# A seventh of the aggregation by a second level of Strassen-Winograd: one of seven products split into seven of half size, in 13 of 16 units

## The chip, the cores and the metric

One core of a Trainium2 chip. The time is device microseconds of one execution, the median over several. The core's engines are named as the profile names them: PE is TensorE (matrix products into PSUM, the banks in which sums are held), DVE is VectorE, ACT is ScalarE, POOL is GpSimd and SP is SyncE. The last two only issue transfers in the stage that is looked at here. Every engine works through its own list of instructions in order; a list that waits holds everything behind it.

## What is computed

Two graph layers over 4096 nodes with 512 features. Everything is f32. The second layer is the larger part, and its last step, the aggregation, is what the change touches.

```python
def _L1_gnn_ref(x, adj, weight, bias, node_w, edge_w):
    ...
    node_att = jax.nn.softmax(x @ node_w, axis=0)
    h = x @ edge_w
    e = h @ h.T
    e = jnp.where(adj > 0, e, NEG_BIG)
    edge_att = jax.nn.softmax(e, axis=1)
    combined_att = node_att * edge_att
    support = x @ weight
    output = adj * combined_att @ support
    return output + bias
...
x = _layernorm(x + _L0_gnn_ref(x, adj, L0_gnn_weight), axis=-1)
x = _layernorm(x + _L1_gnn_ref(x, adj, L1_gnn_weight, ...), axis=-1)
```

## The kernel before

The kernel first does layer 0, then the scores e (4096 x 4096) block by block, which it stores in memory (`s_d`) with running row maxima and sums. The left-hand sides of the aggregation, the columns of the layer's input, are stored in memory too (`lop_d`), already combined for the scheme below. Then comes the stage of the change: it fills the profile from about 1078 us to the end.

The aggregation is cut into 16 units, `Aggregate(g, r)`, with g the outer and r the inner of two indices from 0 to 3. In the code units count n = 0 to 15. Unit (g, r) takes a square of 2 x 2 blocks of attention, each 512 x 512: the block rows r and r + 4, the block columns g and g + 4. A block lies in a buffer of 128 partitions x 4 x 512 (1 MB). There are 13 such buffers, `slot` and `lent`, handed out by `take()` in the order in which they were given back to `free`.

A unit multiplies the 2 x 2 square by a 2 x 2 left-hand side with seven products in place of eight (Strassen's scheme in Winograd's form). The right operands are the blocks r11, r21, r22 and four combinations t1 to t4 of them; the left operands are seven 512 KB slices of `lop_d[r]`, loaded on SP's queue into four buffers `lop` (L883). Each product m has two halves h, and each half is four matmuls of 128x512 into one PSUM bank `ps` (L887) out of a pool of six. After it, VectorE adds the bank to a running sum `total[m, h]` in `over` (L891); where r = 0 there is nothing to add to, and ScalarE copies (L889). Over the four r of one g these seven sums grow; then they are joined (L913), multiplied by the layer's weight (`Finish`, L969, matmuls of 128x256 into `po`), added to the input rows (L980), normalised and stored. That work for group g is queued in `todo` and handed out piece by piece among the products of the next group.

While unit n runs on TensorE, unit n + 1 is prepared, in steps (`steps`) that are handed out one or so after each half product by `between()`: loads of four score blocks on POOL's queue (`load`, L790), loads of four adjacency blocks (`mask`, L797), for each block a shift by the row maximum on VectorE (L803) and its exponential on ScalarE (L804), a weighing by the adjacency in four pieces on VectorE (`weigh`, L810), and last the four combinations (`combine`, L819 to L827). An adjacency buffer is given back after its weighing, and the next adjacency block is loaded then. At the end of a group `panel` makes the row maxima and factors for the next one; it turns them with four transposes on TensorE (L769), through one of two banks of another pool.

A scheduler sets the final order on each engine, from the order in which the code issues the work. So the lists of the built programs are read here, and not the code alone.

Of the kernel before, what the change touches and what calls it, by code (L numbers as in the profile page):

```python
# [11 lines left out]
F32 = mybir.dt.float32  # L12
# [6 lines left out]
P = 128  # L19
# [9 lines left out]
def kernel(  # L29
# [13 lines left out]
    nc = tc.nc  # L43
# [3 lines left out]
    W = 512  # L47
    NG = N // W
    BG = W // P
    HB = NB // 2  # L50
    HG = NG // 2
    HD = D // 2
# [6 lines left out]
    dram = ctx.enter_context(tc.tile_pool(name="dram", bufs=1, space=bass.MemoryType.DRAM))  # L59
# [16 lines left out]


    lop_d = [dram.tile([P, 7, BG, HD], F32, name=f"lop_d{g}") for g in range(HG)]

# [74 lines left out]
    with (  # L156
# [184 lines left out]
        with tc.manual_schedule(engines={mybir.EngineType.DVE, mybir.EngineType.Activation}):  # L341
            for n in range(NB):
                b = n // 2 + n % 2 * HB
# [58 lines left out]
        count = [0]  # L402
# [248 lines left out]
    class Couple:  # L651
# [38 lines left out]
        def quad(self, q, between):  # L690
# [56 lines left out]
            between()  # L747
            yield

    panels = {}  # L750

    def panel(A):

        cols = slice(A * BG, (A + 1) * BG)
        nm = small.tile([P, BG], F32, name="nm")
        nc.vector.tensor_reduce(nm, nmax_c[:, cols, :], AX.X, ALU.min)
        d = small.tile([P, BG, NG], F32, name="d")
        nc.vector.tensor_tensor(d, nm.unsqueeze(2).to_broadcast([P, BG, NG]), nmax_c[:, cols, :], ALU.subtract)
        nc.scalar.activation(d, d, AF.Exp)
        nc.vector.tensor_mul(d, d, sum_c[:, cols, :])  # L760
        f = pan.tile([P, BG], F32, name="f")
        nc.vector.tensor_reduce(f, d, AX.X, ALU.add)
        nc.vector.reciprocal(f, f)
        nc.vector.tensor_mul(f, f, node_att[:, cols])
        spread = rows.tile([P, BG, P], F32, name="spread", tag="rows")
        nc.vector.tensor_copy(spread, nm.unsqueeze(2).to_broadcast([P, BG, P]))
        pt = ps_tr.tile([P, BG, P], F32, name="ptm", tag="tr")
        for i in range(BG):
            nc.tensor.transpose(pt[:, i, :], spread[:, i, :], ident)  # L769
        if A % HG:  # L770
            free_e.append(panels[A - 1][1])
        mrow = take(free_e)
        nc.scalar.copy(mrow.rearrange("p (b w) -> p b w", w=P), pt)
        panels[A] = f, mrow
# [4 lines left out]
    class Aggregate:  # L779
# [46 lines left out]
                self.t4 = take()  # L826
                pinned[0](nc.vector.tensor_sub(self.t4, self.t2, r21))  # L827

        def steps(self):

            self.q, self.a, self.since = [None] * 4, [None] * 4, [None] * 8

            def begin():
                for n in range(2):
                    self.load(n)
                    self.mask(n)
                for n in range(2, 4):
                    self.load(n)

            yield begin  # L840
            yield lambda: self.shift(0)
            yield lambda: self.shift(1)
            for n in range(2):
                yield lambda n=n: self.weigh(n, n + 2)
                yield lambda n=n: self.shift(n + 2)
            yield lambda: self.weigh(2, None)
            yield lambda: self.weigh(3, None)
            for n in range(4):
                yield lambda n=n: self.combine(n)
# [23 lines left out]
                yield landed(n), lambda n=n: self.shift(n)  # L873
                yield landed(4 + n), lambda k=k, n=n: self.weigh(n, order[k + 2] if k < 2 else None)

        def main(self, between):
            r11, t1, r21, r22 = self.q
            total = sums[:, self.g % 2]
            last = self.g == HG - 1 and self.r == HG - 1
            for m in (0, 1, 5, 6, 4, 2, 3) if last else (0, 1, 2, 4, 6, 5, 3):  # L880
                rop = (lambda: r11, lambda: r21, lambda: r22, lambda: self.t4, lambda: t1, lambda: self.t2, lambda: self.t3)[m]()
                lop = lopp.tile([P, BG, HD], F32, name="lop")
                nc.sync.dma_start(lop, lop_d[self.r][:, m])  # L883
                for h in range(2):
                    ps = ps_mm.tile([P, W], F32, name="ps", tag="mm")
                    for c in range(BG):
                        nc.tensor.matmul(ps, lop[:, c, ts(h, P)], rop[:, c, :], start=(c == 0), stop=(c == BG - 1))  # L887
                    if self.r == 0:
                        nc.scalar.copy(total[:, m, h, :], ps)  # L889
                    else:  # L890
                        nc.vector.tensor_add(total[:, m, h, :], total[:, m, h, :], ps)  # L891
                    between()
                free.append(rop)
                if last:
                    for done in self.joins.get(m, ()):
                        join(self.g, done, nc.vector)
# [20 lines left out]
    class Finish:  # L917
# [26 lines left out]
        def pair(self, q, pool):  # L944
            sums_g = sums[:, self.g % 2]
            upper, lower = (sums_g[:, 2], sums_g[:, 4]) if self.half else (sums_g[:, 1], sums_g[:, 3])
            a, b = q, q + 2
            l11, l12, l21, l22 = (x[:, :, ts(i, P)] for i in (a, b) for x in (upper, lower))
            tag = "tr" if pool is ps_tr else "mm"
            bank, s = {}, []  # L950

            def combine():
                s.append(lopp.tile([P, 4, KD // 2, P], F32, name="left1", tag="lop"))
                s1, s2, s3, s4 = (s[0][:, n] for n in range(4))
                nc.vector.tensor_add(s1, l21, l22)
                nc.vector.tensor_sub(s2, s1, l11)
                nc.vector.tensor_sub(s3, l11, l21)
                nc.vector.tensor_sub(s4, l12, s2)

            def multiply(name, lop, rop, *to):  # L960

                first = name not in bank
                if first:
                    x = name == "x"
                    bank[name] = (ps_mm if x else pool).tile([P, HD], F32, name="po", tag="mm" if x else tag)
                po = bank[name]
                lop = lop if not isinstance(lop, int) else s[0][:, lop]
                for k in range(KD // 2):
                    nc.tensor.matmul(  # L969
                        po,  # L970
                        lop[:, k, :],
                        w1_r[rop][:, k, :],
                        start=(first and k == 0),
                        stop=(k == KD // 2 - 1),
                        skip_group_check=not first,
                    )
                f, _ = panels[self.A]
                for i, h in to:
                    xb = self.xbs[i][:, ts(h, HD)]
                    nc.vector.scalar_tensor_tensor(xb, po, f[:, i : i + 1], xb, ALU.mult, ALU.add)  # L980

            def half_stats(i, h):
                if self.last:
                    if i not in self.stats:
                        if not spare:
                            spare.append(take(free_e))
                        at = 64 * (self.half * BG + i)
                        self.stats[i] = spare[0][:, at : at + 12].rearrange("p (h s) -> p h s", h=2)
                    nc.vector.bn_stats(self.stats[i][:, h, :], self.xbs[i][:, ts(h, HD)])
                    if h == (0 if i == b else 1):  # L990
                        self.norm([i])

            yield combine
            yield lambda: multiply("y", l11, 0, (a, 0))
            yield lambda: (multiply("x", l12, 1, (a, 0)), half_stats(a, 0))
            yield lambda: multiply("y", 1, 5, (a, 1))
            yield lambda: multiply("z", 0, 4, (b, 1))
            yield lambda: (multiply("y", 2, 6, (b, 1)), half_stats(b, 1))
            yield lambda: (multiply("z", 3, 2, (a, 1)), half_stats(a, 1))
            yield lambda: (multiply("y", l22, 3, (b, 0)), half_stats(b, 0))  # L1000
# [92 lines left out]
        early_.popleft()[1]()  # L1093
    reclaim()
    todo = deque()


    over = big.tile([P, KD * N], F32, name="over", tag="large")
# [8 lines left out]

    for n, u in enumerate(blocks):
        nxt = blocks[n + 1] if n + 1 < len(blocks) else None
        first = deque()  # L1110
        pinned[0] = tc.keep_in_program_order if n == 0 else lambda ins: ins
        if n == 0:
            first.extend(f for _, f in early_)
            first.extend(lambda n=n: u.combine(n) for n in range(4))
        if nxt:
            first.extend(nxt.steps())
            if n:
                first.popleft()()
            if u.r == HG - 1:
                first.extendleft([lambda: panel(nxt.g + HG), lambda: panel(nxt.g)])  # L1120
# [6 lines left out]

        def between():
            count[0] += 1
            for queue, share in ((first, -(-len(first) // (15 - count[0]))), (todo, 1)):  # L1130
                for _ in range(min(share, len(queue))):
                    queue.popleft()()

        u.main(between)
        assert not first
        if u.r == HG - 1 and nxt:
            todo.extend(lambda g=u.g, n=n: join(g, n, nc.vector) for n in range(7))
# [4 lines left out]
    assert not todo  # L1142

    for e in ends_:
        for steps in zip(e.pair(0, ps_tr), e.pair(1, ps_mm)):
            for step in steps:
                step()

# [36 lines left out]
```

## Time and profile before

| what | us |
|---|---|
| median of 6 runs | 1957.35 |
| lowest and highest of them | 1954.27, 1960.07 |
| the profiled execution | 1954.27 |
| its span | 1952.5 |
| VectorE busy in it | 1386.9 |
| ScalarE busy in it | 694.2 |

The profiled execution is the lowest of the six, and its span is what the instructions cover; the rest of its time lies around them. A busy TensorE is not a TensorE at its peak, since matmuls are pipelined and the ends of their records are modelled: a row's mean (592 ns for 128x512) is longer than the step from one matmul to the next. An f32 matmul leaves two records. The costliest groups of the stage, with line, engine, operation, output and input, count, then busy time in us, mean ns, idle time before them and what ended it:

```profile
L887 PE MATMUL ps<-lent,lop 128*128 128x512 f32 x960 | 423.4, 592 | 0.0
L887 PE MATMUL ps<-slot,lop 128*128 128x512 f32 x832 | 365.7, 592 | 0.0
L891 DVE TENSOR_TENSOR over<-over,ps 128x512 f32<-128x512 f32 x168 | 114.1, 682 | 101.9 <-PE ps L887 101.9
L803 DVE CUSTOM_DVE_ANT_1 lent<-lent,line 128x2048 f32<-128x2048 f32 x32 | 73.1, 2287 | 26.2 <-DMA lent<-s_d 26.2
L803 DVE CUSTOM_DVE_ANT_1 slot<-slot,line 128x2048 f32<-128x2048 f32 x32 | 73.0, 2287 | 20.0 <-DMA slot<-s_d 18.7
```

The stage's transfers (queue, operation, count, size of one, median us from issue to landing):

```profile
lop<-lop_d SPq DMA_DIRECT2D x112, 512.0 KB, 3.9
slot<-s_d POOLq DMA_DIRECT2D x32, 1024.0 KB, 6.7
lent<-s_d POOLq DMA_DIRECT2D x32, 1024.0 KB, 7.4
```

### The profile page before, as it was taken

The page shows a single profiled execution, that of the slowest core. Times are in us where ns is not written, and L with a number is a line of the kernel's source. Part 1 is how long each engine was busy: PE and PEld are TensorE (multiplying, and loading weights), DVE is VectorE, ACT ScalarE, POOL GpSimd, SP SyncE. Part 2 cuts the span into 40 slices and gives each one's busy share as a digit, 9 for nine tenths or more (in the row PEclk, how much of TensorE's full clock was granted, in tenths as well). Part 3 has the DMA queues.
Part 4 walks back from the last instruction along what each step waited for, and adds up shares of the span by engine and source line. Part 5 has one row for each costly group of instructions (what it writes and reads, how often), then busy time and mean ns, then how long its engine had stood idle before and what let it go on. Part 6 is the DMA issues. An engine that isn't in the chain of part 4 may idle for free.

```text
span 1952.5 us, 18709 instructions
## 1 busy us (share of the span) xinstructions
PE 1939.3 (99%) x6314; PEld 1124.9 (58%) x6314; DVE 1386.9 (71%) x2154; ACT 694.2 (36%) x1134; POOL 326.1 (17%) x472
## 2 busy tenths in 40 slices
PE   9999999999999999999999999999999999999998
PEld 6888888888544445455555444445544555445545
DVE  7767666676774576567565896987769766988637
ACT  5433333333203576677677420221222220331100
POOL 0122222122441111011122211111111110211100
PEclk9999999999999999999999999999999999999999
DMA  9898888888385577578679977775777765776631
GB/s 312 296 326 311 294 324 312 303 318 309 122 298 191 183 263 296 197 272 284 240 297 326 336 279 267 257 251 192 249 247 262 246 244 192 282 248 215 215 97 43
DMA packets 134064, 497.75 MB, mean 255 GB/s; under 512 B 13904, under 2 KB 13904, under 8 KB 126288
## 3 DMA queue, kind: packets, MB, share of 16 engines
q0 software_dynamic: 70752, 260.08, 35.4%
q1 hardware_dynamic: 54864, 207.12, 31.8%
q10 hardware_dynamic: 8352, 29.36, 4.2%
q8 instruction: 50, 0.82, 0.2%
q14 instruction: 46, 0.38, 0.1%
HBM read 376.96 MB, written 119.54 MB: 254 GB/s over the span
## 4 chain that ended last, share of the span: by engine, by line
PE 93%; DMA 2%; issue 2%; DVE 1%; ACT 1%; POOL 0%; POOLq 0%; DVEq 0%; ACTq 0%
PE ps L887 39%; PE seven L699 12%; PE acc L371 11%; PE acc L370 11%; PE seven L98 5%; PE po L969 5%; PE pe L630 4%; PE pt L600 2%; DMA s_d<-slot 2%; PE acc L243 1%; PE pw L211 1%; PE pt L330 1%; ACT line L571 1%; PE acc L244 1%; PE idle L197 0%
## 5 line engine op out<-in xcount | busy, mean ns | idle before, releaser
L887 PE MATMUL ps<-lent,lop 128*128 128x512 f32 x960 | 423.4, 592 | 0.0
L370 PE MATMUL acc<-xw,hi 128*128 128x512 f32 x960 | 376.4, 392 | 0.0
L371 PE MATMUL acc<-xw,lo 128*128 128x512 f32 x960 | 374.2, 390 | 0.0
L887 PE MATMUL ps<-slot,lop 128*128 128x512 f32 x832 | 365.7, 592 | 0.0
L887 PEld LDWEIGHTS ps<-lent,lop 128*128 128x128 f32 x960 | 182.0, 190 | 205.4 <-issue 200.9
L887 PEld LDWEIGHTS ps<-slot,lop 128*128 128x128 f32 x832 | 157.8, 190 | 183.8 <-issue 179.4
L362 DVE TENSOR_TENSOR lo<-at,hi 128x1024 fp32r<-128x1024 f32 x120 | 146.9, 1224 | 85.2 <-ACT hi L360 85.2
L371 PEld LDWEIGHTS acc<-xw,lo 128*128 128x128 f32 x960 | 180.3, 188 | 37.1 <-DVE lo L362 0.3
L370 PEld LDWEIGHTS acc<-xw,hi 128*128 128x128 f32 x960 | 180.3, 188 | 36.8
L360 ACT CAST hi<-at 128x1024 fp32r<-128x1024 f32 x120 | 126.4, 1054 | 203.4 <-PE acc L370 151.0
L891 DVE TENSOR_TENSOR over<-over,ps 128x512 f32<-128x512 f32 x168 | 114.1, 682 | 101.9 <-PE ps L887 101.9
L804 ACT ACTIVATE lent<-lent 128x2048 f32<-128x2048 f32 x32 | 61.2, 1912 | 212.7 <-DVE lent L803 212.7
L630 PE MATMUL pe<-hT 128*128 128x512 f32 (+3 forms) x384 | 132.1, 486 | 0.0
L562 DVE CUSTOM_DVE_ANT_0 line<-lent,slot 128x512 f32<-128x512 bf16 x144 | 93.0, 687 | 45.9 <-ACT slot L640 23.0
L571 ACT ACTIVATE line<-line,nmax_c 128x512 f32<-128x512 f32 x160 | 114.8, 724 | 22.2 <-DVE nmax_c L562 22.1
L803 DVE CUSTOM_DVE_ANT_1 lent<-lent,line 128x2048 f32<-128x2048 f32 x32 | 73.1, 2287 | 26.2 <-DMA lent<-s_d 26.2
L699 PE MATMUL seven<-hT 128*128 128x512 f32 x192 | 89.8, 593 | 0.0
L804 ACT ACTIVATE slot<-slot 128x2048 f32<-128x2048 f32 x32 | 61.2, 1911 | 77.7 <-DVE slot L803 72.8
L630 PEld LDWEIGHTS pe<-hT 128*128 128x128 f32 x384 | 64.6, 191 | 41.4 <-issue 33.8
L803 DVE CUSTOM_DVE_ANT_1 slot<-slot,line 128x2048 f32<-128x2048 f32 x32 | 73.0, 2287 | 20.0 <-DMA slot<-s_d 18.7
L600 PEld LDWEIGHTS pt<-ident,lent 128*128 128x128 f32 x412 | 51.2, 141 | 52.9 <-issue 38.9
L601 ACT COPY slot<-pt 128x512 f32<-128x512 f32 (+3 forms) x126 | 69.5, 554 | 27.0 <-PE pt L600 23.2
(228 smaller groups left out, 2565.8 us busy)
## 6 DMA issues: line engine op xcount, KB each, us to landing
at<-in_adj_t_dram SPq DMA_DIRECT2D x60, 1024.0 KB, 7.0
lop<-lop_d SPq DMA_DIRECT2D x112, 512.0 KB, 3.9
lent<-in_adj_t_dram POOLq DMA_DIRECT2D x34, 1024.0 KB, 6.6
s_d<-slot POOLq DMA_DIRECT2D x33, 1024.0 KB, 7.0
slot<-s_d POOLq DMA_DIRECT2D x32, 1024.0 KB, 6.7
lent<-s_d POOLq DMA_DIRECT2D x32, 1024.0 KB, 7.4
slot<-in_adj_t_dram POOLq DMA_DIRECT2D x30, 1024.0 KB, 6.8
lent<-in_adj_dram SPq DMA_DIRECT2D x48, 512.0 KB, 5.1
```

The source lines that it names most:

```text
L98: nc.tensor.matmul(banks[bank][q], lop(m, q)[k], rop(m)[k], start=(first and k == 0), stop=(k == K - 1), skip_group_check=not first,)
L360: nc.scalar.copy(hi, aq)
L362: nc.vector.tensor_sub(lo, aq, hi.bitcast(F32))
L370: nc.tensor.matmul(acc, hi[:, c, :], xw[:, kb, :], start=(kb == 0), stop=False)
L371: nc.tensor.matmul(acc, lo[:, c, :], xw[:, kb, :], start=False, stop=(kb == NB - 1))
L571: nc.scalar.activation(line, line, AF.Exp, bias=nmax_c[:, b, c : c + 1], scale=-1.0, accum_out=sum_c[:, b, c : c + 1])
L630: nc.tensor.matmul(pe[:, lo * P :], hT[:, k, ts(A * BG + i, P)], hT[:, k, (B * BG + lo) * P : (B + 1) * W], start=(k == 0), stop=(k == KD ...
L699: nc.tensor.matmul(ps, left[m][:, k, q, :], right[m][:, k, :], start=(first and k == 0), stop=(k == KD // 2 - 1), skip_group_check=not first,)
L803: pinned[0](nc.vector._custom_dve(TENSOR_ADD_SAT, out=q, in0=q, in1=m, s0=0.0, s1=-HUGE))
L804: nc.scalar.activation(q, q, AF.Exp)
L887: nc.tensor.matmul(ps, lop[:, c, ts(h, P)], rop[:, c, :], start=(c == 0), stop=(c == BG - 1))
L891: nc.vector.tensor_add(total[:, m, h, :], total[:, m, h, :], ps)
```

## The change

In units 2 to 14 (`two`), product 0 of the seven, r11 by its left-hand side, is no longer done as two halves of four matmuls. It is cut once more into a 2 x 2 square and done by the same scheme with seven products of half size, each two matmuls of 128x256: 14 matmuls of 128x256 in place of eight of 128x512. The other six products stay and count 12 turns; after each turn one piece of the seventh is issued (`beside`).

- The right side: four differences of 128x2x256 on VectorE in turns 1 to 4, one of them in place (r12), three into a buffer `right` taken at the unit's start.
- The left side: the raw slice of `lop_d` is loaded on SP's queue into a buffer taken in turn 2, and its four combinations with it. The first time that an r comes up (units 2 to 5) the combinations are made on VectorE and stored to the new `lop2_d[r]`; the other nine times they are loaded from there.
- The seven half-size products come in turns 5 to 11. They run through two banks: y takes four of them on top of each other, and x and z, the two halves of the other bank, take the rest. After each one VectorE adds the running bank into a quarter of the sum of product 0; where r = 0, the first write of each quarter is a copy on ScalarE.
- To make room, the load of the next unit's fourth score block moves from the unit's start to turn 4.
- The six banks are made once and handed out by hand in turn (`next_bank`); while a half-size chain runs it holds two of them, and the other products turn through four. The panels' transposes and part of the last `Finish` go through the same ring. The steps of the next unit are spread over 12 turns, where it was 14.

```diff
+    def next_bank():
+        banks.rotate(-1)
+        return banks[-1]
...
+        def second(self, nxt):
...
+            r = self.q[0]
+            (r11, r12), (r21, r22) = [[r[:, k : k + h, c : c + w] for c in (0, w)] for k in (0, h)]
+            total = sums[:, self.g % 2, 0]
+            c = {f"{k + 1}{n + 1}": total[:, k, n * w : n * w + w] for k in range(2) for n in range(2)}
+            new = set(c) if self.r == 0 else set()
+            right = take()
...
+            def load():
+                left = l["buf"] = take()
...
+                nc.sync.dma_start(raw, lop_d[self.r][:, 0])
+                if not fresh:
+                    nc.sync.dma_start(left[:, h:, :], lop2_d[self.r])
...
+            def multiply(name, lop, rop, *to):
+                first = name not in bank
+                if first:
+                    if name == "z":
+                        bank["z"] = bank["x"][:, w:]
+                    else:
+                        bank[name] = banks.popleft()
+                ps = bank[name][:, :w]
...
+                for k in range(h):
+                    nc.tensor.matmul(ps, lop[:, k, :], rop[:, k, :], start=(first and k == 0), ...)
+                for n in to:
+                    if n in new:
+                        new.remove(n)
+                        nc.scalar.copy(c[n], ps)
+                    else:
+                        nc.vector.tensor_add(c[n], c[n], ps)
...
+            return {
+                1: [lambda: nc.vector.tensor_sub(t3, r22, r12)],
+                2: [load, lambda: nc.vector.tensor_sub(r12, r12, r11)],
+                3: [lambda: nc.vector.tensor_sub(t2, r22, r12)],
+                4: [(lambda: nxt.load(3)) if nxt else (lambda: None), lambda: nc.vector.tensor_sub(t4, r21, t2), combine],
+                5: [lambda: multiply("y", "11", r11, "11")],
+                6: [lambda: multiply("x", "12", r21, "11")],
+                7: [lambda: multiply("y", 2, t2, "12")],
+                8: [lambda: multiply("z", 1, r12, "22")],
+                9: [lambda: multiply("y", 3, t3, "22")],
+                10: [lambda: multiply("z", 4, r22, "12")],
+                11: [end],
+            }
...
-            for m in (0, 1, 5, 6, 4, 2, 3) if last else (0, 1, 2, 4, 6, 5, 3):
+            beside = self.second(nxt) if two else {}
+            turn = 0
+            for m in (0, 1, 5, 6, 4, 2, 3) if last else (1, 2, 4, 6, 5, 3) if two else (0, 1, 2, 4, 6, 5, 3):
...
-                    ps = ps_mm.tile([P, W], F32, name="ps", tag="mm")
+                    ps = next_bank()
...
+                    turn += 1
+                    if h:
+                        free.append(rop)
+                    for act in beside.get(turn, ()):
+                        act()
...
+        two = 2 <= n < len(blocks) - 1
```

## The prediction, made before the changed kernel ran

> **What bounds the kernel now.** I read the page's first part and its chain first, then windows of one unit and a bit (54.3 us) over the aggregation stage (1078 us to the end), then the chain in order of time, and last the rows that price what the change adds.
>
> ```profile
> span 1952.5 us, 18709 instructions
> PE 1939.3 (99%) x6314; PEld 1124.9 (58%) x6314; DVE 1386.9 (71%) x2154; ACT 694.2 (36%) x1134; POOL 326.1 (17%) x472
> PE 93%; DMA 2%; issue 2%; DVE 1%; ACT 1%; POOL 0%; POOLq 0%; DVEq 0%; ACTq 0%
> ```
>
> Three windows (columns: PE, PEld, DVE, ACT and POOL busy with counts, granted clock, DMA share, GB/s):
>
> ```profile
> 1349.90:1404.20 54.30, 54.30 (x147) 27.66 (x146) 38.92 (x64) 14.72 (x12) 10.34 (x16) 1.00 0.64 227
> 1458.50:1512.80 54.30, 54.30 (x128) 24.02 (x127) 53.80 (x60) 15.21 (x13) 7.49 (x10) 1.00 0.72 249
> 1512.80:1567.10 54.30, 54.30 (x148) 27.82 (x147) 42.33 (x50) 11.51 (x12) 5.99 (x8) 1.00 0.69 238
> ```
>
> TensorE has no idle time in the stage, at a granted clock of 1.00. VectorE is the runner-up: 38.9 us of 54.3 in an ordinary stretch, 53.8 where a group ends (there it also joins the seven sums and makes the panels), 42.3 after it. So work taken off TensorE shortens the kernel, as long as VectorE, which gets more, doesn't fall behind. The price of TensorE's work, from the chain in order of time (start, length, what):
>
> ```profile
> 1873.86 48.07 PE ps L887 x112
> 1921.92 19.87 PE po L969 x92
> L969 PEld LDWEIGHTS po<-over x128: 190/190/190, 1304.5 to 1936.9; 128*128 128x128 f32 x128
> L969 PE MATMUL po<-over x128: 379/379/379, 1304.9 to 1937.1; 128*128 128x256 f32 x128
> ```
>
> The first line is one whole unit: 7 products, 112 records (an f32 product of 128x512 leaves two), 0.429 us a record. The second is the same for 128x256: 0.216 us. The rows' 592 and 379 ns contain pipelining and are not the step.
>
> **TensorE's share of the change.** Removed in each of 13 units: one product of 16 records, 16 x 0.429 = 6.87 us. Added: seven half-size products, each of two products of 128x256, so four records: 28 x 0.216 = 6.05 us. Gain 0.82 us a unit, 10.65 us in 13. That the loads stay hidden is read from the row: a load takes 0.190 us and the step was 0.216. Break-even is 6.87 / 28 = 0.245 us a record.
>
> The Trainium skill, "TensorE: Matmul & The Clock Gate", Part 3 on packing small matmuls, states that a weight load overlaps matmuls in flight "only when row_grp differs"; all loads here are of the full 128x128. By that rule a unit would lose 28 x 0.406 - 16 x 0.619 = 1.46 us, the kernel 19 us. The trace says otherwise: 92 steps with their loads took 19.87 us, and 112 took 48.07.
>
> **VectorE's share.** The rows, with what stands in the order around them:
>
> ```profile
> 1477.01 2.28 DVE L824 TENSOR_TENSOR slot<-slot,slot 128x2048 f32<-128x2048 f32 x1
> 1479.22 0.68 DVE L891 TENSOR_TENSOR over<-over,ps 128x512 f32<-128x512 f32 x1
> 1479.81 2.28 DVE L827 TENSOR_TENSOR lent<-slot,slot 128x2048 f32<-128x2048 f32 x1
> 1482.02 0.68 DVE L891 TENSOR_TENSOR over<-over,ps 128x512 f32<-128x512 f32 x1
> 1482.61 2.28 DVE L803 CUSTOM_DVE_ANT_1 lent<-lent,line 128x2048 f32<-128x2048 f32 x1
> 1458.85 2.49 DVE L810 SCALAR_TENSOR_TENSOR slot<-lent,slot 128x512 f32<-128x512 f32 x4
> L955 DVE TENSOR_TENSOR left<-over 128x256 f32<-128x256 f32 x16 | 6.7, 417 | 0.0
> L1122 DVE TENSOR_TENSOR line<-over 128x512 f32<-128x512 f32 x1 | 0.7, 693 | 4.4 <-DMA over<-in_w_dram 4.4
> ```
>
> A unit with r > 0 holds 4 shifts (9.1), 16 weighs in fours (10.0), 4 combines (9.1) and 14 adds (9.5): 37.7 us of 48.07. Added: four differences of 2x256 columns, which is the shape of L1122, 4 x 0.69 = 2.8; eight adds of 128x256 out of PSUM, which no row has. Bounds: 0.42 (L955, same shape, from SBUF) and 0.48 (L980, 128x256 from PSUM with a scalar). I take 0.42, since L891 from PSUM (0.68) costs what L1122 costs from SBUF (0.69): 3.3 us. Removed: two adds of 0.68. Net 4.8 us (5.3 at the upper bound). With r = 0 four half sums are ScalarE copies, and two full ones left ScalarE before: net 2.8 + 1.7 = 4.5. The first use of each r (units 2 to 5) makes four left-hand sums, 1.7 us more. Over 13 units: 10 x 4.8 + 3 x 4.5 + 4 x 1.7 = 68 us. The twelve windows from 1187.0 to 1838.6 hold 505.6 us of VectorE in 651.6; so 574 in 641 remains, 90%. VectorE has room for it as a whole, not everywhere.
>
> **What waits.** Of six banks two go to the half products, so a bank is wanted again after three products, not five: 3 x 3.43 us and about two half products, 12 us, where it was 17. The reading of the group's end above shows adds of 0.68 every 2.8 us behind one combine or shift each; against 12 us that is cover. The two running half sums (y, and x whose other half is z) are tighter: each half product waits for the add of the one before it in its bank, two turns earlier, 2 x 3.43 + 0.86 = 7.7 us; between stand at most a shift, four weighs and an add (2.29 + 2.49 + 0.68 = 5.5). No wait, where the halves really come one a turn. In the built order of the changed kernel exactly one full product stands between any two halves in units 2 to 6, 9, 10, 13 and 14, and nearly so in 8 and 12 (one pair adjoins). In units 7 and 11, where groups 1 and 2 end, the panels crowd VectorE, and the last four halves come with half a product between them or less than one (0 to 0.75). From the four weighs that free the buffer of the adjacency until z's first half is added, the order has: reload of that buffer, four weighs, half add: 6.8 (page, slot<-in_adj_t, 1024 KB) + 2.49 + 0.42 = 9.7 us. On TensorE, in the same stretch, stand six matmuls of 128x512 (0.859 each, two records) and three half products (0.864), 7.75 us, before z's second half, which needs that add. Wait: 2.0 us each, 4.0 for both. Bounds: 0, if VectorE is ahead; with single reloads of this kind at 5.6 to 10.4 us in the trace, up to 5.6 each, 11 for both, all of the gain. I take the median.
>
> **What moves at no cost I can see.** The load of the fourth score block goes from the start of a unit to turn 4 on POOL's queue, into the buffer that the second product gives back: 4 x 3.43 = 13.7 us into the unit, landing 6.7 to 7.4 us later (page), 21 us. Its shift stands on VectorE at turn 6, 6 x 3.43 + two halves = 22.3 us. It is 1.3 us early; a slow landing (10.4) holds VectorE 2 us, with the adds behind it, and the ring of 12 us covers TensorE. On SP the half product's left side (512 KB) goes into the buffer that the first product frees, so SP waits up to 6.9 us, then a second load of 512 KB; the page's 3.9 us each makes 14.7 us, and the first half is wanted after turn 5, 17.2 us. Behind the wait stand the loads of later products; four buffers keep them three products ahead, 10 us or more. Nine extra loads and four stores of 512 KB are 6.8 MB of 497.75, DMA share 0.64 to 0.72. The panels' transposes move into the ring; the unit count and the last unit stay.
>
> **Sum.** 10.65 - 4.0 = 6.65 us. The profiled execution took 1954.27 us, 1.8 over its span, and is the lowest of six; it would become 1947.6. The median stands 3.1 us higher, 1957.35, so 1950.7 us is the forecast, 0.34%; 1946.7 if nothing waits. A measurement of this kernel can tell 0.2%, 3.9 us, from no change.
>
> **Rivals.** *The waits eat it.* The half sums' chain waits wherever a reload lands late, not in two units alone: 0.3 us to 1.1 us in each of 13 units (4 to 14 us), so 1951 to 1961, about 1957. For it: VectorE already waits for score blocks (L803 for s_d: 26.2 and 18.7 us in 64), and now half adds stand behind such waits. Against: the 7.7 us above.
> *VectorE becomes the bound.* Place: units 7/8 and 11/12, and 3/4. VectorE has 0.5 us left in 54.3 there, and gets 4.8 + 4.5 in about two units, some 9 us it must be late by; the halved ring holds 12, and the lateness also takes the next unit's operands. It decides from where the lateness passes 12 us, so if the added operations cost a third more than I take, or the backlog isn't gone (12 us idle in the next window, 7 after the change) by the next end. Then about 9 us show at each of three ends: 28 - 10.65, 17 us slower, 1975; with half of it 1961.
> *It doesn't do what it says:* the half products' step is above 0.245 us, because their operands come from strided quarters of buffers. Against: L969 reads quarters as well. 0.26 us would give 1957.35 + 13 x 0.4 = 1963.
>
> **How the numbers follow.** Forecast 0.66 (1946 to 1953.4), the waits eat it 0.18 (taken as within 3.9 us), VectorE 0.13, step 0.03. So faster 0.66, same 0.18, slower 0.16. The range runs from the gain without waits (10.65, and 0.7 for the median's own scatter) to the end of "same": 1946 to 1961; the forecast's own is 1946 to 1953.4.
>
> **What would show it.** Records of the halves 0.216 us apart; the stage's windows still at full PE; VectorE about 48 us of 54 in ordinary windows; PE's waits for VectorE a few us in all, at the ends of groups 1 and 2. Wrong if TensorE waits for a half add in most units, or if VectorE's full windows spread to two in a row with gaps in PE.

## The result, and the profile after

The changed kernel is a little slower: 1961.5 us median of 23 runs (1956.31 to 1973.74), beside 1957.22 us for the kernel before (48 runs). The ratio is 1.0024, 95% interval 1.0016 to 1.0032. The forecast was 1950.7. The profiled execution took 1957.13 us, 1.8 over its span, and is one of the shortest of the 23.

The page of the changed kernel, in the places shown of before: the engines, the shares of the chain that ended last, the costliest groups, the transfers.

```profile
span 1955.3 us, 19195 instructions
PE 1930.8 (99%) x6470; PEld 1153.5 (59%) x6470; DVE 1436.2 (73%) x2281; ACT 694.5 (36%) x1140; POOL 326.0 (17%) x472
PE 81%; DMA 7%; issue 6%; DVE 3%; POOL 1%; ACT 1%; POOLq 0%; DVEq 0%; SPq 0%; ACTq 0%
L981 PE MATMUL bank<-slot,lop 128*128 128x512 f32 x800 | 356.2, 592 | 0.0
L985 DVE TENSOR_TENSOR over<-over,bank 128x512 f32<-128x512 f32 x148 | 100.6, 681 | 67.7 <-PE bank L981 67.7
lop<-lop_d SPq DMA_DIRECT2D x99, 512.0 KB, 5.3
slot<-s_d POOLq DMA_DIRECT2D x37, 1024.0 KB, 7.4
lent<-s_d POOLq DMA_DIRECT2D x27, 1024.0 KB, 8.9
```

TensorE has less work, and the chain has left it: 81% of the span where it was 93%, and transfers have come in with 7%. VectorE's adds wait 67.7 us for banks where they waited 101.9, and the stage's transfers land 0.7 to 1.5 us later. The stage is as long as before: 868.8 us from the first record of its products (1079.9 us) to TensorE's last (1948.7), and the same in the kernel before (1077.3 to 1946.1). Counted from the starts of TensorE's records in the stage, against steps of 0.429 us for 128x512 and 0.215 for 128x256, it runs 10.7 us late in all in the changed kernel and 0.1 in the kernel before. So the 10.65 us that it has less to do came back as waits inside the stage. The windows of 54.3 us show where (the columns are those of before):

```profile
1404.20:1458.50 54.30, 51.69 (x155) 29.14 (x154) 35.55 (x56) 3.19 (x2) 4.49 (x6) 1.00 0.63 221
1458.50:1512.80 54.30, 53.10 (x146) 26.50 (x145) 49.38 (x64) 21.06 (x23) 11.10 (x17) 1.00 0.74 263
1512.80:1567.10 54.30, 54.30 (x158) 29.70 (x157) 51.98 (x65) 14.03 (x15) 6.74 (x9) 1.00 0.78 273
```

TensorE is full in most. It is short above all in the window with the second half of unit 6 and the first of unit 7, where VectorE is at 35.55 of 54.3 and so far from full, and a little in the next, with the rest of unit 7. The waits of TensorE in the stage, by what was waited for (us in total, times, longest), are one line; before, this view was empty:

```profile
PE bank L932 <- DVE over L945: 8.7, 5, 2.6
```

A half product (L932) waits five times for VectorE's add of a half product (L945): 2.61 us in unit 6, 1.95 in unit 10, 2.55 in unit 14, and 1.16 and 0.43 in units 7 and 11. The four records behind each wait take 1.13 us in the chain below, where they take 0.86 elsewhere, so the loss is some 10 us rather than 8.7. The chain of waits, in order of time, says what came ahead of the adds, in units 6 and 7:

```profile
1391.60 6.31 DMA out_dram<-xb
...
1398.19 0.53 POOL xb L1039
1398.72 8.68 DMA slot<-s_d
...
1407.42 2.29 DVE slot L815
1409.71 0.34 DVE over L945
...
1410.10 1.13 PE bank L932 x4
...
1415.53 0.86 PE bank L932 x4
...
1479.53 5.79 DMA slot<-in_adj_t_dram
...
1485.41 2.50 DVE slot L822 x4
1487.91 0.34 DVE over L945
...
1488.30 1.13 PE bank L932 x4
```

In unit 6 the last group's finished rows are stored (out_dram), the next input rows (xb) want the stored rows' buffers, and POOL's queue stands for the stores. Behind the rows stands the fourth score block, issued at 1398.72, 20.6 us into the unit (its first product starts at 1378.1). It lands 8.68 us later, VectorE shifts it, and only then does it reach the half add that TensorE wants. In unit 7 it is the chain that the prediction had named: reload of an adjacency block, four weighs, half add. The same view prices the halves: four records of 128x256 in 0.86 us.

### The profile page after: what moved, and what is told of

The parts are those of the page before. It is cut to its first block, busy times and chain, and to the rows that moved or that the text cites. A ratio compares the mean times of both kernels' runs of the same rounds, so it can differ in the third digit from the quotient of the medians.

```text
span 1955.3 us, 19195 instructions
## 1 busy us (share of the span) xinstructions
PE 1930.8 (99%) x6470; PEld 1153.5 (59%) x6470; DVE 1436.2 (73%) x2281; ACT 694.5 (36%) x1140; POOL 326.0 (17%) x472
## 4 chain that ended last, share of the span: by engine, by line
PE 81%; DMA 7%; issue 6%; DVE 3%; POOL 1%; ACT 1%; POOLq 0%; DVEq 0%; SPq 0%; ACTq 0%
PE bank L981 27%; PE seven L701 12%; PE acc L373 11%; PE acc L372 11%; PE pe L632 4%; PE seven L100 4%; PE bank L932 3%; PE po L1066 3%; PE pt L602 2%; DMA s_d<-slot 2%; DMA out_dram<-xb 1%; DMA slot<-s_d 1%; PE bank L1066 1%; PE acc L245 1%; PE pw L213 1%
## 5 line engine op out<-in xcount | busy, mean ns | idle before, releaser
L981 PE MATMUL bank<-slot,lop 128*128 128x512 f32 x800 | 356.2, 592 | 0.0
L981 PE MATMUL bank<-lent,lop 128*128 128x512 f32 x784 | 348.7, 592 | 0.0
L981 PEld LDWEIGHTS bank<-slot,lop 128*128 128x128 f32 x800 | 151.6, 190 | 162.8 <-issue 157.8
L981 PEld LDWEIGHTS bank<-lent,lop 128*128 128x128 f32 x784 | 148.8, 190 | 160.1 <-issue 154.7
L816 ACT ACTIVATE slot<-slot 128x2048 f32<-128x2048 f32 x37 | 70.6, 1910 | 260.2 <-DVE slot L815 249.7
L985 DVE TENSOR_TENSOR over<-over,bank 128x512 f32<-128x512 f32 x148 | 100.6, 681 | 67.7 <-PE bank L981 67.7
L815 DVE CUSTOM_DVE_ANT_1 slot<-slot,line 128x2048 f32<-128x2048 f32 x37 | 84.5, 2285 | 25.0 <-DMA slot<-s_d 25.0
L816 ACT ACTIVATE lent<-lent 128x2048 f32<-128x2048 f32 x27 | 51.6, 1911 | 99.9 <-DVE lent L815 99.9
L1111 ACT ACTIVATE rstd<-mv,eps 128x1 f32<-128x1 f32 (+1 forms) x14 | 4.1, 296 | 187.4 <-DVE mv L1108 143.0
```

Of the source, the lines that this page charges most:

```text
L816: nc.scalar.activation(q, q, AF.Exp)
```

## The experiments

Each kernel was compared with the kernel before on the same chip. What a theory's letter stands for is said in each expectation; a letter belongs to the runs it was written for.

**The ring alone (e1).** No unit is cut; the ring of banks stays, and the pace and the place of the load are those of before.

```diff
-        two = 2 <= n < len(blocks) - 1
+        two = False
```

> No unit is cut; of the change only the banks handed out by hand and the panels' transposes in that ring stay. Theory A (the cut saves its 10.65 us and the waits of the half products, 10.3 us in the profile, take it back): this kernel takes the time of the one before, 1957.2 us, ratio within 0.1% of 1. Rival C (the ring itself, or where things lie in memory, costs some 4 us whatever the halves do): 1960 to 1962 us, ratio 1.0015 to 1.0025.

Measured: 1956.76 us, ratio 1.0000 (0.9991 to 1.0009). Handing out the banks by hand costs nothing.

**The fourth block on another queue (e2), and at the unit's start again (e3).** e2 issues the load at turn 4 on SP's queue. e3 puts it back at the unit's start; the buffer for the differences is then taken in turn 2, the left side is loaded in turn 4, and the halves run a turn later, 6 to 12.

```diff
-                4: [(lambda: nxt.load(3)) if nxt else ...
+                4: [(lambda: nxt.load(3, nc.sync)) if nxt else ...
```

```diff
-                if not beside:
-                    self.load(3)
+                self.load(3)
...
+                2: [make],
+                3: [lambda: nc.vector.tensor_sub(v["t3"], r22, r12)],
+                4: [load, lambda: nc.vector.tensor_sub(r12, r12, r11)],
...
+                12: [end],
```

> The changed kernel, but the load of the next unit's fourth score block is issued on SP's queue in place of POOL's; place in the program and buffer are the same. Theory A (in units 6, 10 and 14 this load stands on POOL's queue behind the stores and input rows of the group's end, lands late, and holds the half sums behind its shift): the waits of 2.9, 2.2 and 2.8 us in those units go, those in units 7 and 11 (2.4 us) stay, so 7.9 us less than the change, 1953 to 1954 us. Rival B (VectorE has too much work, and the wait shows wherever it is late): the waits come back in other units, 1960 to 1962 us.

> The changed kernel with the fourth score block loaded at the start of the unit again, as before the change; for that the buffer of the right-hand differences is taken in turn 2 and the left side loaded in turn 4, and the half products come in turns 6 to 12. Theory A: as with the load on SP's queue the waits of units 6, 10 and 14 go, 1953 to 1954 us, unless the left side now comes late (turn 4 plus two loads of 5 us against turn 6), which would show as waits for a DMA on TensorE. Rival B: no faster than 1960 us.

Measured: e2 1957.63 us, ratio 0.9999 (0.9988 to 1.0010); e3 1956.06 us, 0.9996 (0.9985 to 1.0007). Each takes back about a quarter of a per cent against the changed kernel, and each stops at the time of the kernel before. TensorE's waits of e2 over the stage:

```profile
PE po L1066 <- DVE xb L1077: 6.1, 3, 2.7
PE bank L932 <- DVE over L945: 1.5, 2, 1.0
```

and of e3:

```profile
PE po L1069 <- DVE xb L1080: 7.3, 3, 3.1
```

The waits for half adds in units 6, 10 and 14 are gone, and in the same three units the products with the layer's weight (`po`) wait for the add to the input rows instead. Who waited for the stores (out_dram) in e3 explains these rows:

```profile
  POOL xb L1042: 44.5, 14
```

In the kernel before this line reads 3.2 us, in the changed one 19.9. In e3 four blocks of 1 MB, three of scores and one of adjacency, are issued just ahead of the stores, at 1380.1 to 1382.3 us; the last store, issued at 1387.63, takes 13.2 us to land, and the row loads come at 1397.5 to 1401.7. So the first late transfer had hidden a second one.

**The units at a group's end left whole (e4).** Units 3, 7 and 11 are not cut.

```diff
-        two = 2 <= n < len(blocks) - 1
+        two = 2 <= n < len(blocks) - 1 and u.r != HG - 1
```

> The changed kernel with the last unit of each group (units 3, 7 and 11) left uncut. Theory A: three units lose 0.82 us of gain each (2.5 us) and the waits of units 7 and 11 (2.4 us) go: the time of the change, 1961 to 1962 us, with the waits of units 6, 10 and 14 still there. Rival B: VectorE is relieved by 4.8 us just where it is fullest, and most waits go with it: 1953 to 1956 us.

Measured: 1964.06 us, ratio 1.0027 (1.0013 to 1.0041). The waits of units 7 and 11 went, and those of 6, 10 and 14 stayed (1.88, 4.59 and 2.07 us). These ends are not where the gain is lost.

**Work of the halves left out (e6, e7).** In e6 the half products are not added to the sums where a running sum exists. In e7 the four right-hand differences are not made, and r22 stands in for t2, t3 and t4.

```diff
-                    else:
-                        nc.vector.tensor_add(c[n], c[n], ps)
```

```diff
-            t2, t3, t4 = right[:, :h, :w], right[:, :h, w:], right[:, h:, :w]
+            t2 = t3 = t4 = r22
...
-                1: [lambda: nc.vector.tensor_sub(t3, r22, r12)],
```

> The changed kernel with the half products' adds on VectorE left out (79 of 128x256 out of PSUM; the copies on ScalarE stay), so product 0's sum is not what it should be, and TensorE never waits for such an add. Theory A (it is the chain of half sums that waits, one add behind a late shift): nearly the whole gain shows, 1947 to 1951 us. Rival B (VectorE's total): 33 us less on VectorE, the same as leaving out the differences, 1950 to 1955 us. If waits move to the po chain, as in the two runs with an earlier load, 1953 to 1956 us.

> The changed kernel with the four differences of the right side on VectorE left out in every cut unit (52 of 128x2x256, 2.8 us a unit, 36 us; the half products take r22 in their place), so product 0 is not what it should be. The half adds and the chain through the two banks stay. Theory A (late transfers and the chain): the waits of the half sums stay, 1958 to 1962 us. Rival B (VectorE's total): as without the half adds, 1950 to 1955 us.

Measured: e6 1966.31 us, ratio 1.0045 (1.0028 to 1.0062); e7 1955.08 us, 0.9993 (0.9981 to 1.0005). e6 says little of the half adds. The scheduler set other orders, and TensorE's waits in the stage are for input rows and for a left side on SP's queue:

```profile
PE po L1064 <- DVE xb L1075: 6.2, 4, 2.6
PE bank L932 <- DMA lent<-lop_d: 3.7, 1, 3.7
```

e7 has 30 us less on VectorE (1406.3 us on its page after 1436.2) and takes back about as much as e2 and e3. Theory A missed: of the waits for half adds only 1.1 us in unit 7 is left, and rows for `po` make TensorE wait 5.4 us in units 6, 10 and 14. In unit 6 the fourth block goes out later still, at 1400.78, 24.3 us into the unit, and VectorE stands 4.7 us for it; but in this order a half add comes ahead of its shift (at 1401.73, the shift at 1407.81). So a late block need not cost a wait where the half add stands ahead of its shift. e7 changes VectorE's work and its order at once, and can't tell which of the two did it. Less work by itself doesn't bring the whole gain back.

**The input rows on SP's queue (e5), and both places mended (e8).** e8 is e3 with this line:

```diff
-                nc.gpsimd.dma_start(xb, rows_[ts(i, P), :])
+                nc.sync.dma_start(xb, rows_[ts(i, P), :])
```

> The changed kernel with the input rows of the group's end (x1 into xb, four transfers of 256 KB per half of a group) loaded on SP's queue in place of POOL's. Theory A (POOL's queue stands still while these four loads wait for the stores of the half before, which use the same buffers; the score and adjacency blocks behind them come late, VectorE waits for those in order, and the half sums wait behind it): the waits of units 6, 10 and 14 go, 8 us less than the change, 1953 to 1955 us. Rival B (VectorE is too full): 1959 to 1962 us, with the waits elsewhere.

> Both repairs together: the fourth score block loaded at the unit's start (as in the run of that name) and the input rows on SP's queue. Theory A: nothing of the group's end stands before a block on POOL's queue and the po chain's rows come in time, so most of the 10.65 us shows, 1948 to 1952 us, faster than both kernels. Rival B: 1956 to 1958 us, as with the load at the start alone.

Measured: e5 1963.64 us, ratio 1.0026 (1.0016 to 1.0037); e8 1951.41 us, 0.9962 (0.9949 to 0.9976). Alone, moving the rows moves the waits and no more, and theory A missed. The block no longer stands behind them, and the waits for half adds fall from 8.7 to 1.2 us; but the rows still come late, in unit 6 VectorE stands 6.4 us for them, and `po` waits 10.7 us in all. Together with the block at the unit's start it makes the one version faster than both kernels; counted as above, TensorE is late by 3.5 us in e8's stage, where it was 10.7.

**The pace of the group's work (e9 to e12).** In the kernel before, the work of a group's end goes out at 14 steps a unit, in the changed one at 12; at 1389.5 us the stores of unit 6 come 11 us after the unit's start, where they came 4.5 us ahead of it. e9 goes back to 14 a unit, e10 is that with e3, e11 that with e8, e12 goes to 11.

```diff
+            more = 2 if two and count[0] % 6 == 0 else 1
-            for queue, share in ((first, ...), (todo, 1)):
+            for queue, share in ((first, ...), (todo, more)):
```

> The changed kernel, with two steps of the group's end handed out in turns 6 and 12 of a cut unit, so that a unit hands out 14 of the 43 steps again, as before the change, and not 12. Theory P (the pace: at 12 a unit the first half's stores and the second half's rows fall 11 us into unit 6, behind the burst of block loads, where they fell 5 us ahead of it; and the panels of unit 7 wait for row buffers until step 43): the waits of units 6, 10, 14, 7 and 11 (10.3 us in the profile of the change) go, and the time is 1948 to 1952 us, with the fourth block still loaded in turn 4 on POOL's queue. Rival A (the late load of the fourth block is the cause by itself): waits stay where its shift comes late, 1955 to 1960 us. Rival B (VectorE's total): 1958 us and more.

> The kernel with the fourth block loaded at the start (median 1956.1 us when it ran alone) with 14 steps a unit. Theory P: 1948 to 1951 us, no faster than the pace alone by more than 2 us. Rival A: clearly faster than the pace alone, by 4 us or more.

> Load at the start, rows on SP's queue, and 14 steps a unit. If the pace is what both repairs worked around, this adds little to either: 1947 to 1951 us. All of the 10.65 us would be 1947.

> The changed kernel with 11 steps of the group's end a unit in place of 12 (none in turn 12): the suspected cost made larger. Theory P: the group's end runs still later, its last step falls near the end of units 7 and 11, the panels with it, and the waits grow: 1964 us or more. Theory A or B: as the change, 1960 to 1963 us.

Measured: e9 1962.45 us, ratio 1.0024 (1.0013 to 1.0035); e10 1963.36, 1.0031 (1.0020 to 1.0041); e11 1964.78, 1.0041 (1.0029 to 1.0053); e12 1965.14, 1.0038 (1.0026 to 1.0050). The pace isn't the cause: a slower one is at most a little worse (its interval overlaps that of the change), and the faster one mends nothing, and spoils the version that was mended. In e10 all of TensorE's waits are the panels', in e11 9.0 of 11.6 us. The chain of e10 in unit 7:

```profile
1443.70 8.49 DMA out_dram<-xb
...
1452.28 0.44 DVE spread L775
...
1452.77 1.97 PE bank L781 x8
```

The stores now come just behind three block loads on POOL's queue (1435.8 to 1439.9), take 8.49 us, and the panel's input on VectorE waits for them, with TensorE's transposes behind it: 9.2 us in two waits.

**Is it VectorE's fullness? (e13, e14, e15)** These change the kernel before, which has no half products and no wait in the stage. e13 adds twelve in-place maxima of 128x256 a unit, e14 moves the load of the fourth block to turn 4, e15 does both.

```diff
+                    turn += 1
+                    if more and turn <= 12:
+                        part = total[:, m, h, : W // 2]
+                        nc.vector.tensor_tensor(part, part, part, ALU.max)
```

```diff
-                for n in range(2, 4):
-                    self.load(n)
+                self.load(2)
+                if not late:
+                    self.load(3)
...
+            if count[0] == 4 and nxt and n >= 2:
+                nxt.load(3)
```

> The kernel before, with twelve in-place maxima of 128x256 added on VectorE in each of units 2 to 14 (about 0.42 us each, 5 us a unit, 65 us in all, what the change adds there); TensorE's work, the banks and every transfer stay as before. Theory F (VectorE is full: its work and the waits for late blocks that it takes in order leave no cover) expects TensorE to begin to wait, several us in the stage, although there is no half product and no late block: 1960 to 1966 us, ratio 1.0015 to 1.0045. Theory C (the waits belong to the half products' chain through two banks, or to the block loaded at turn 4) expects nothing: ratio within 0.001 of 1, and TensorE full in the stage.

> The kernel before, with nothing but the load of the fourth score block moved from the unit's start to turn 4 in units 2 and on. Theory F expects little: VectorE has some 10 us in 54 left there to make up for it, ratio 0.9995 to 1.001. Theory L (the late block by itself makes the waits) expects TensorE to wait in units 6, 10 and 14, where the load stands behind the stores of the group before: 2 to 3 us each, ratio 1.003 to 1.005.

> The kernel before, with both: the filler of 5 us a unit on VectorE and the fourth block at turn 4. Theory F expects more than the filler alone, since the two eat the same cover: ratio 1.003 to 1.007, 1963 to 1971 us. Theory C (the half products' chain through two banks) expects no wait here either, ratio within 0.001 of 1; theory L expects the same as the late load alone.

Measured: e13 1957.26 us, ratio 1.0001 (0.9992 to 1.0009); e14 1974.23 us, 1.0082 (1.0068 to 1.0096); e15 1960.64 us, 1.0013 (1.0004 to 1.0023). VectorE's busy time in e13 is 1436.6 us, as in the changed kernel. Its windows at the end of group 1:

```profile
1458.50:1512.80 54.30, 54.30 (x128) 24.10 (x127) 54.30 (x66) 14.28 (x12) 6.45 (x9) 1.00 0.67 242
1512.80:1567.10 54.30, 54.30 (x146) 27.45 (x145) 49.71 (x70) 12.71 (x14) 7.49 (x10) 1.00 0.73 258
```

VectorE has no idle time in the first and 4.6 us in the second, and TensorE is full in both. Theory F falls for the kernel with six banks in turn. With the ring of four, e8 answers it: it has all of the change's work on VectorE (1434.6 us) and waits 1.2 us. e14 has not one operation more than the kernel before and loses 16 us. TensorE's main waits in it (a panel's of 1.2 us stands beside them), then VectorE's order in unit 6 (start, length, what, and in brackets the idle time ahead and what ended it):

```profile
PE po L970 <- DVE xb L981: 13.5, 4, 4.9
```

```profile
1385.50 0.48 DVE L981 SCALAR_TENSOR_TENSOR xb<-po,f,xb 128x256 f32<-128x256 f32 x1 [5.99 <-DMA xb<-x_d]
1393.72 2.29 DVE L803 CUSTOM_DVE_ANT_1 lent<-lent,line 128x2048 f32<-128x2048 f32 x1 [7.73 <-DMA lent<-s_d]
...
1399.31 0.69 DVE L810 SCALAR_TENSOR_TENSOR lent<-slot,lent 128x512 f32<-128x512 f32 x1 [1.71 <-ACT lent L804]
1399.92 0.48 DVE L981 SCALAR_TENSOR_TENSOR xb<-po,f,xb 128x256 f32<-128x256 f32 x1
```

VectorE stands for a score block while row adds wait behind it; TensorE, idle for 4.49 us, goes on at 1400.45, after the last one shown, which stands behind a weighing of that block too. Theory L named the right units and too small a loss. The edit moves more than one load: by the built programs, adjacency blocks go ahead of score blocks on POOL's queue, buffers change hands, and VectorE's list is another one. So 16 us is the price of the edit with its new order, not of a late block as such. That it falls to 0.13% when the filler is added, which makes another order again, says the same.

**What makes the block late, and whose gain e8 is (e16, e17, e18).** e16 repeats e8. e17 and e18 put the input rows on SP's queue in the kernel before and in e14.

> The same kernel as in e8 once more (the changed kernel, with the fourth block loaded at the unit's start, and the group's input rows loaded on SP's queue). If its gain is one of the kernel and not of that day's runs, the ratio is again 0.995 to 0.9975, about 1951 us.

> The kernel before, with nothing but the loads of a group's input rows (xb) moved from POOL's queue to SP's. TensorE has no wait in the stage before, so if the gain of e8 and e16 is that of the half products, nothing is gained here: ratio 0.9992 to 1.0008. Rival G (the gain of e8 and e16 is that of the moved rows and has little to do with the half products): ratio 0.998 or below. If the rows make SP's loads late, TensorE waits for lop: ratio above 1.001.

> The kernel of e14 (before, with the fourth block loaded at turn 4), and the input rows on SP's queue as well. Theory Q (the block is late because of what stands ahead of it on POOL's queue where a group's rows and stores are issued: in e14, at unit 6, rows that waited 3.8 us for stores to land, then the block that VectorE stood 7.7 us for) expects most of e14's 16 us to go: ratio 0.999 to 1.003. Rival B (it is late because of the buffer that it waits for, whatever stands ahead) expects TensorE's waits in units 6, 10 and 14 to stay: ratio 1.005 to 1.009.

Measured: e16 1950.64 us, ratio 0.9966 (0.9954 to 0.9977); e17 1958.43 us, 1.0013 (1.0004 to 1.0022); e18 1975.29 us, 1.0098 (1.0084 to 1.0112). The gain of e8 stands. It isn't the moved rows', which cost 0.13% by themselves. Theory Q falls: with the rows off POOL's queue e14's loss stays, so what stands ahead of the block there isn't the reason in that kernel. For the changed kernel this doesn't follow: there the chain shown above runs through the stores and rows, and e5 took most of the waits for half adds away. e2 says it most directly: on SP's queue the same load, into the same kind of buffer, goes out 14.0 us into unit 6 (1392.77, the unit starts at 1378.8), and not 20.6. The waits left in e16:

```profile
PE bank L935 <- DVE over L948: 1.6, 3, 1.1
PE po L1069 <- DVE xb L1080: 0.7, 2, 0.4
```

## Why the prediction was wrong, point by point

- **TensorE's share: right.** Four half records in 0.86 us are 0.215 each, forecast 0.216. Unit 2 takes 47.2 us between first products, 48.1 before. With the waits nearly gone, e8 and e16 show 0.38% and 0.34%, 7 us, of the 10.65. The rule of the Trainium skill that spoke against it ("TensorE: Matmul & The Clock Gate", Part 3: a load overlaps matmuls in flight only when row_grp differs) doesn't hold here: loads of the full array, 0.190 us each, stayed hidden in steps of 0.215.
- **VectorE's share: too high, without effect.** Forecast 68 us more, measured 49.3 on the page. Eight half adds a unit were counted and the code makes seven (79 in all, by the instructions that e6 lacks), some 5 us of the difference. For the rest, durations were added, and back to back the records overlap: in the kernel before, adds of 128x256 of 0.42 us start at 1403.28, 1403.61 and 1403.95, 0.33 apart.
- **"VectorE becomes the bound": fell.** e13 fills the same window that was named and loses nothing with six banks, and e8, with all of the change's work and the ring of four, waits 1.2 us.
- **Waits in units 7 and 11, 4.0 us: right mechanism, smaller.** Measured 1.16 + 0.43 us, through the very chain that was written down.
- **"What moves at no cost I can see": the step that failed.** The load at turn 4 was put at 13.7 us into the unit, landing by 21, needed at 22.3. In units 6, 10 and 14 it cost 2.61, 1.95 and 2.55 us of waits, 7.1 in all. In unit 6 it was issued at 20.6 us (1398.72, the unit starts at 1378.1), landed at 29.3, and the half add came at 31.6. The buffer was not what held it, since on SP's queue, in e2, it was issued at 14.0 us, close to the forecast. The prediction listed what stood ahead on SP's queue and not on POOL's: four stores and four row loads in the unit where the group before stores its first half. e2, which issues this load alone on another queue, and e3, which puts it back at the unit's start with the halves a turn later, take the waits at the half adds of these units away.
- **"The ring of 12 us covers TensorE": failed with it.** The add behind the late block was not one of the ring's but one of the half products' chain, for which the prediction itself had only 7.7 us.
- **A second term was not seen at all.** With the block mended, the rows behind the slow stores take the same three units (e2, e3: 6.1 and 7.3 us). Only with both mended does the gain come out (e8, e16).
- **The median.** The rival "the waits eat it" names the half sums' chain, and 1957 us, which is the profiled execution's time; but it saw a wait in each of 13 units, and there were five, in units 6, 7, 10, 11 and 14. The median is 4.4 us above that execution. Executions of the changed kernel list their mean granted clock: 0.999 for the profiled one, 0.996 for most of those from 1961.5 to 1965.1, 0.993 for the longest, 1973.74. The 0.003 between the first two are 5.9 of 1957 us. So the typical execution loses more to the clock than the one that was profiled. In e2 and e11 waits of 2.69 and 2.01 us, about as long as those of units 6, 10 and 14, are followed by a halved clock that costs about 1.7 us more each (below); three such would be 5 us, an estimate. That this happened in these executions isn't shown, since there is no profile of them.

**Open.** Up to the stage's first product the profiled execution of the changed kernel is 2.6 us behind, as are those of e2 and e3, but not those of e1 and e4; e13, which has nothing of the change, is 3.7 us behind there, so the cut need not be the reason. This wasn't traced further. Every edit reorders VectorE's and POOL's lists, so no run changes one wait alone. That the late block and the rows are one cause each, which add up, rests on e2, e3, e5 and e8 together; why e14 loses as much as 16 us is known only as far as its order shows. An order written by hand, the load moved and nothing else, wasn't tried.

## What to carry to other kernels

Before a load is moved to a later place, write down for each kind of unit, above all those in which the phase before is still being finished and stored, everything that its queue issues ahead of it and what that waits for, and who stands behind its consumer on an in-order engine; an engine with 19 us to spare in 54 can still be late with the one add that matters. A busy sum is the wrong test: 50 us of extra work cost nothing, and a moved load, with the order that came with it, cost 16. When mending one wait brings another of the same size in the same place, look for the second late transfer before giving up the idea, since here only both mends together showed the gain.

## What the runs showed of the hardware

**A wait can cost more than its length, and its length alone doesn't tell when.** In the profiled execution of the changed kernel waits of up to 2.61 us left the granted clock at 1.00 in the 4 us windows around them. In e18 a wait of 4.98 us is followed by slow matmuls. TensorE's timeline in unit 10, and the windows there (granted clock third from the end):

```profile
1608.03 1.03 PE L970 MATMUL po<-over 128*128 128x256 f32 x4
1608.89 3.60 PE L888 MATMUL ps<-lent,lop 128*128 128x512 f32 x8
1617.47 2.07 PE L970 MATMUL po<-line,left 128*128 128x256 f32 x4 [4.98 <-DVE xb L981]
1619.34 4.96 PE L888 MATMUL ps<-slot,lop 128*128 128x512 f32 x8
```

```profile
1616.00:1620.00 4.00, 2.53 (x5) 1.83 (x6) 2.40 (x4) 2.91 (x2) 0.00 (x0) 0.50 1.03 397
1620.00:1624.00 4.00, 4.00 (x8) 1.71 (x7) 3.49 (x6) 0.28 (x1) 0.75 (x1) 0.74 0.48 181
```

The four records take 2.07 us where they took 1.03, the next eight 4.96 where they took 3.60: 2.4 us on top of the wait, at a clock down to 0.50. The Trainium skill, "TensorE: Matmul & The Clock Gate", Part 1, says that the clock is halved after an idle window of about 3.4 us and full again after a busy one; these two waits agree with it. Others don't: after a wait of 3.71 us in e14 (unit 14) the clock stayed at 1.00, and in e11 one of 2.01 us was followed by a loss of the same kind, as TensorE's timeline and the window show:

```profile
1388.27 1.13 PE L1069 MATMUL po<-line,left 128*128 128x256 f32 x4 [2.01 <-DVE xb L1080]
1389.24 5.29 PE L984 MATMUL bank<-slot,lop 128*128 128x512 f32 x8
```

```profile
1388.00:1392.00 4.00, 3.73 (x8) 2.07 (x9) 4.00 (x6) 0.00 (x0) 0.00 (x0) 0.71 1.03 387
```

The eight records take 5.29 us and not 3.60, so the wait of 2.01 costs 1.7 us more; in e2 one of 2.69 us costs about as much more, at a clock of 0.68 in the 4 us from 1404. What decides besides the length, no run here shows.

**Stores among block loads land late.** In the kernel before a store of 256 KB lands after 2.0 to 3.8 us. In e3, where four blocks of 1 MB are issued on the same queue in the 5.4 us ahead of the stores of unit 6, the last of these takes 13.2 us, and the longest of the stage, in unit 14, 16.6. The share of the DMA engines there is 0.99 to 1.03 in windows of 4 us, where it was 0.58 as the kernel before issued its stores. In e2 only one block goes out on that queue in the 10 us ahead of the same stores, and they take 10.8 to 11.6 us, at a share of 0.81 to 1.04. So many blocks on the stores' own queue aren't needed for it; how the loss divides between that queue and the DMA engines, no run here tells.
